# Two counters and one type: step weights of a hot pass (2 to 4), a layer's pacing point (0.88 to 0.94), and node keys in fp32

## The chip, the core and the metric

The kernel runs on one core of one Trainium2 chip. The core has five engines with a queue of instructions each, and each queue runs in order: PE (TensorE, matrix products), DVE (VectorE), ACT (ScalarE), POOL (GpSimd) and SP (SyncE, which here only issues transfers). An instruction that waits holds up everything behind it on its own engine and nothing else; engines meet at semaphores. SBUF is the working memory of 128 partitions, PSUM holds the results of products, and transfers between HBM and SBUF run on 16 DMA engines. The metric is the device time of one execution in microseconds (us).

## The reference, cut to what matters

There are 12,500 nodes with 256 numbers each and 200,000 edges, sorted by target. A graph convolution of three layers is followed by a feed-forward block on the half of the nodes that a router scores highest:

```
x = x + gcn(layernorm(x))          # three layers, gelu between them
x = x + ffn(layernorm(x))          # the top half of the rows

def _gcn_layer(x, src, dst, norm, W, b, n_nodes):
    h = x @ W
    msg = h[src] * norm[:, None]
    out = jax.ops.segment_sum(msg, dst, num_segments=n_nodes)
    return out + b
```

`dst` is 12500 u^2 with u uniform, so the low nodes have very many edges and the high ones few. The costly part of a layer is `segment_sum` of `h[src]`: 200,000 rows of 256 numbers picked by index.

## The kernel before, in words

**Blocks and tables.** The nodes stand in NB = 98 blocks of 128. The table of a layer holds each node's row as three bf16 parts side by side (PARTS x D = 768 numbers, 1536 bytes), which together have the precision of fp32.

**Two ways to sum.** The first blocks (12, 16 and 8 in the three layers) are "hot" and are done densely: a matrix of counts (how often source l feeds target j) times the whole table. All edges from there on are gathered: a group is four tiles of 128 edges. For each tile `sum_groups` issues one indirect DMA on POOL (L955), which fetches 128 table rows into a buffer `m`; there are 30 such buffers in layers 0 and 1, 20 in layer 2. DVE makes a one-hot matrix `oh` of the targets (L962), PE multiplies it with the rows (L968, twelve products a group), and two DVE instructions add the product in PSUM to a ring of block sums (L978, `here` and `there`). Layer 0 gathers 1027 tiles (257 groups), layer 1 943 (236 groups), layer 2 1127 (282 groups).

**Building the counts.** `build_counts(p)` makes the counts for the four target blocks of hot pass p and stores them to HBM. For each block w it lists the sources of each node by an indirect DMA on POOL (L1014), splits a source into its place and its block on DVE, turns both by a product, and keeps them as `keys` (L1059, written at L1049). Then it compares keys with constant rows: `low_h` (L1084, place, 128 values x up to 4 edges) and `high_h` (L1086, block, 98 or 196 values x up to 4 edges). The pair is multiplied on PE (L1053, "a count product"), and ACT copies the finished counts from PSUM (L1098). Blocks 5 and up are "paired": one instruction covers two edges of each node. Block 0 has more edges than the others and comes in 16 chunks; for its high columns the compares have one edge each (128x128 and 128x98), and they are few. `low_h` and `high_h` have 6 buffers in layer 0 and 3 in layer 1. Build 0 has 160 wide pairs of compares (128x512 with 128x392) and 62 narrow ones, build 1 has 32 with 128x392 and 48 with 128x784, builds 2 and 3 have 64 each with 128x784. Builds 0, 1 and 2 run in layer 0, build 3 in layer 1, none in layer 2.

**Multiplying the counts.** `hot_pass(i, p)` runs over the 98 table blocks; SP loads `t_row` (192 KB, L1128, 5 buffers) and every seventh block `t_cols` (896 KB, L1120, 2 buffers). For each block and each half of the columns three products of 128x512 are issued (L1132), and then the generator yields. There are 3, 4 and 2 passes in the three layers.

**What sets the order.** The instructions are written out by a loop over the groups, and the dense work is laid between them. After each tile of a group `sum_groups` calls `beside` (L1313 and on) with the share of the layer's groups that are done. `beside` takes steps from `all_parts` until the weights of the steps taken reach `share / 0.88` of the layer's whole `cost` (0.55 in layer 2). A step's weight is what the generator yields: 2 for a listing, 1 for a count product, 2 for three products of a pass:

```
                while done < min(1.0, share / (0.88 if i < 2 else 0.55)) * cost:
                    step = next(it, None)
                    if step is None:
                        break
                    done += step
```

`cost` adds `pass_cost = 4 * NB + 4 + WB` = 400 for each pass and `build_cost` for each build (742, 328, 264, 264), in layer 1 also 8 for a check of the order. `all_parts` runs build k beside pass k-1, in proportion to their costs; build 0 has no pass beside it, and the last pass of a layer no build. `beside` also advances the lane of finished rows (`go_on`, every second call): `next_rows` takes the sums of two blocks, applies the layer's end and the next layer's product (L795), and stores the next table. Rows that are left at the end of a layer follow after its last group, and the first gather of the next layer waits for their store.

Of the kernel before, what the change touches and what calls it, by code (L numbers as in the profile page):

```python
# [9 lines left out]
F32 = mybir.dt.float32  # L10
BF16 = mybir.dt.bfloat16
# [6 lines left out]
P = 128  # L18
# [4 lines left out]
NB = (N + P - 1) // P  # L23
# [27 lines left out]
WB = 4  # L51
# [41 lines left out]
def kernel(  # L93
# [911 lines left out]
    def build_counts(p, turn, work, keep, hot, unit, ps_u):  # L1005

        if True:
# [47 lines left out]
            for w in range(p * WB, (p + 1) * WB):  # L1055
                paired = w >= PAIRED
                chunks = CHUNKS if w == 0 else (U if paired else P,)
                first_col = [sum(chunks[:c]) for c in range(len(chunks))]
                keys = keep.tile([P, 2, sum(chunks)], BF16, name="keys0" if w == 0 else "keys", bufs=1 if w == 0 else 2)  # L1059
                for c, m in enumerate(chunks):  # L1060
                    listed(w, c, P if paired else m, keys[:, :, first_col[c] : first_col[c] + m])
                    yield 2
                per = 2 if paired else 1
                width = per * NB
                values = iota_2 if paired else iota_g
                for h in range(2):
                    a = unit.tile([P, NB, U], BF16, name="a")
                    for j in range(0, U, GT * per):
                        col = (h * U + j) // per
                        many = sum(m > col for m in chunks) > 4  # L1070
                        places = {}
                        for k0 in range(0, GT, GT // per):
                            pa = ps_u.tile([P, NB, 4], F32, name="pa")
                            for k in range(k0, k0 + GT // per):
                                if k not in places:
                                    most = 1 if many else GT
                                    for c, m in enumerate(chunks):
                                        n = min(most, m - col - k)
                                        if n <= 0:
                                            break  # L1080
                                        at = first_col[c] + col + k
                                        key = lambda q, v: keys[:, q, None, at : at + n].to_broadcast([P, v, n])
                                        low = hot.tile([P, P, GT], BF16, name="low_h")
                                        nc.vector.tensor_tensor(low[:, :, :n], key(0, P), iota_1[:, :, :n], OP.is_equal)  # L1084
                                        high = hot.tile([P, 2 * NB, GT], BF16, name="high_h")
                                        nc.vector.tensor_tensor(  # L1086
                                            high[:, :width, :n], key(1, width), values[:, :width, :n], OP.is_equal
                                        )
                                        for q in range(n):
                                            places.setdefault(k + q, []).append((low[:, :, q], high[:, :width, q]))  # L1090
                                        if many:
                                            one(pa, k - k0, per, places[k][-1], c == 0, col + k >= max(chunks[c + 1 :], default=0))
                                        yield 1 if many else 0
                                if not many:
                                    for c, hots in enumerate(places[k]):
                                        one(pa, k - k0, per, hots, c == 0, c == len(places[k]) - 1)
                                        yield 1
                            nc.scalar.copy(a[:, :, j + k0 * per : j + k0 * per + 4], pa)  # L1098
                            if len(places[k0]) > 2:
                                top = hot.tile([P, 1], F32, name="top")  # L1100
                                nc.vector.tensor_reduce(top, pa.rearrange("p n j -> p (n j)"), AX.X, OP.max)
                                nc.vector.scalar_tensor_tensor(
                                    bad[:, 6:7], top, 255.0, bad[:, 6:7], op0=OP.is_gt, op1=OP.max
                                )
                    nc.vector.tensor_tensor(a[:, w, :], a[:, w, :], ident[:, h * U : (h + 1) * U], OP.add)
                    nc.sync.dma_start(
                        counts[w // WB][:, :, w % WB * 2 + h, :].rearrange("c l x -> l c x"),
                        a.rearrange("p (c n) j -> p c (n j)", c=NS),
                    )

    def hot_pass(i, p, turn, dones, rows_p, cols_p, back, ps):

        if True:
            sums = [ps.tile([P, WB * P], F32, name=f"sum{h}") for h in range(2)]
            t_cols = {}

            def load(c):
                if c < NS:
                    t_cols[c] = cols_p.tile([P, 2 * WB, HB, U], BF16, name="t_cols")
                    nc.sync.dma_start(t_cols[c].rearrange("p u n j -> p u (n j)"), counts[p][c])  # L1120

            load(0)
            for c in range(NS):
                load(c + 1)
                for n in range(HB):
                    t_row = rows_p.tile([P, PARTS * D], BF16, name="t_row")
                    b = c * HB + n
                    nc.sync.dma_start(t_row, tables[i][b * P : (b + 1) * P, :])  # L1128
                    for h in range(2):
                        for part in range(PARTS):  # L1130
                            f = part * D + h * P
                            nc.tensor.matmul(  # L1132
                                sums[h], t_row[:, f : f + P], t_cols[c][:, :, n, :],
                                start=(b == 0 and part == 0), stop=(b == NB - 1 and part == PARTS - 1),
                            )
                        yield 2
            for h in range(2):
                turned = back.tile([P, WB * P], F32, name=f"turned{h}")
                nc.scalar.copy(turned, sums[h])
                sums[h] = turned  # L1140
                yield 2
            for k in range(0, WB, 2):
                pk = turn.tile([P, 2, DC, P], F32, name="pt")
                for j in range(2):
                    for h in range(2):
                        nc.tensor.transpose(pk[:, j, h, :], sums[h][:, (k + j) * P : (k + j + 1) * P], ident)
                done = dones.tile([P, 2, D], F32, name="done")
                nc.vector.tensor_copy(done.rearrange("p n d -> p (n d)"), pk.rearrange("p n c d -> p (n c d)"))
                yield 2
                yield (p * WB + k, 2, ("whole", done))  # L1150
# [60 lines left out]
    def layer(i):  # L1211
# [10 lines left out]
        with ExitStack() as s:  # L1222
            w = layer_weights(s, i)
# [9 lines left out]
            pools = layer_pools(h, (30, 30, 20)[i])  # L1233
            for_pass = pass_pools(h)
            for_build = build_pools(h, (6, 3)[i]) if made else None
            pass_cost = 4 * NB + 4 + WB

            def all_parts():

# [4 lines left out]
                while passes or builds:  # L1244
                    b = p = None
                    b_cost = p_cost = 0
                    if builds:
                        k, b_cost = builds.pop(0)
                        b = build_counts(k, mine[1], *for_build)
# [27 lines left out]
            cost = PASSES[i] * pass_cost + sum(build_cost(before_now + k) for k in range(made)) + (8 if i == 1 else 0)  # L1277
            it = all_parts()
            done = 0
# [33 lines left out]
            def beside(g, share):  # L1313
                nonlocal done, slot, junk_at
                if junk_at is not None and g >= junk_at:
                    junk_at = None
                    b0 = junk[0]
                    for b in range(b0, b0 + junk[1], 2):
                        clear(b, 2, ring)
                while done < min(1.0, share / (0.88 if i < 2 else 0.55)) * cost:  # L1320
                    step = next(it, None)
                    if step is None:
                        break
                    done += step
                slot += 1
                if i == 2 or slot % 2 == 0:
                    go_on(g)
                if i == 2 and (slot % 2 == 0 or len([x for x in ffns if not x[4]]) > 1):
                    ffn_on()
# [209 lines left out]
    with tc.tile_pool(name="flag", bufs=1) as work, tc.tile_pool(  # L1539
        name="ps_flag", bufs=1, space=bass.MemoryType.PSUM  # L1540
# [41 lines left out]
```

## Time and profile before

| what | value |
|---|---|
| median of 13 runs | 4653.12 us (4646.86 to 4667.55) |
| the profiled execution | 4652.44 us |
| its span, first to last instruction | 4650.5 us |
| PE busy | 3811.1 us (82%) |
| DVE busy | 2178.5 us (47%) |
| ACT busy | 1064.6 us (23%) |
| POOL busy | 3219.1 us (69%) |
| gathers of layer 0, first and last start | 235 to 1680 us |
| gathers of layer 1 | 1744 to 2960 us |
| gathers of layer 2 | 3015 to 4483 us |
| mean granted TensorE clock | 0.912 |

How to read it: a row of a group says line, engine, operation, output and inputs, shapes and the number of instructions, then the busy time in us and the mean of one in ns, and then the idle time of the engine just before them with what ended it. A view by stretches gives, for each stretch, the busy time of every engine with its number of instructions in brackets, then the granted TensorE clock, the busy share of the DMA engines and GB/s. Instructions of one engine overlap by some 75 ns where they follow each other at once, so sums of durations are a little above busy time.

### The profile page before, as it was taken

To read this page: it belongs to the slowest core of one execution; us is meant where nothing else is said; L and a number is where in the kernel's file an instruction comes from. 1 tells how busy PE (TensorE), PEld (TensorE's weight loads), DVE (VectorE), ACT (ScalarE), POOL (GpSimd) and SP (SyncE) were. 2 spreads that over 40 slices of the span, in tenths; PEclk is the share of its full clock that TensorE was granted. 3 is DMA by queue.
4 is the path that set the end of the run, shared out by engine and by line. 5 is a ranking of instruction groups with operands and counts; after the bars stand their busy time and mean duration, and the time that the engine had idled before them with its cause. 6 is when DMAs were issued, how large, how long until landed. Compare 5 with 4: busy or idle time off the path is not lost. (4 is left out here: it accounts for less than half of the span.)

```text
span 4650.5 us, 64287 instructions
## 1 busy us (share of the span) xinstructions
PE 3811.1 (82%) x21815; PEld 2731.4 (59%) x21815; DVE 2178.5 (47%) x5972; ACT 1064.6 (23%) x2187; POOL 3219.1 (69%) x3329
## 2 busy tenths in 40 slices
PE   5757669989798857888999988578999999888966
PEld 4635446656455544555556655345767778777755
DVE  8767545555443443444333334333343445455556
ACT  6602222333221121222111111201121113223311
POOL 4477777777766737777777777477776777777740
PEclk9968889999899978998999999789999999999978
DMA  5746678989898847899999998578877776666648
GB/s 165 256 124 183 211 234 302 325 292 337 292 323 298 267 147 251 284 294 322 337 324 338 334 320 262 157 233 253 261 240 232 257 247 196 194 198 198 200 130 295
DMA packets 591308, 1176.38 MB, mean 253 GB/s; under 512 B 78368, under 2 KB 403128, under 8 KB 590968
## 3 DMA queue, kind: packets, MB, share of 16 engines
q0 software_dynamic: 199200, 610.24, 42.5%
q1 hardware_dynamic: 285910, 460.42, 28.6%
q10 hardware_dynamic: 105858, 101.52, 6.6%
q8 instruction: 173, 2.83, 0.2%
q14 instruction: 167, 1.37, 0.1%
HBM read 988.29 MB, written 183.59 MB: 252 GB/s over the span
## 5 line engine op out<-in xcount | busy, mean ns | idle before, releaser
L955 POOL DMA_INDIRECT m<-table,idx x3097 | 3073.8, 992 | 1199.2 <-issue 440.8
L968 PE MATMUL pm<-m,oh 128*128 128x256 bf16 x9291 | 1503.8, 289 | 524.0 <-DMA m<-table,idx 380.9
L968 PEld LDWEIGHTS <-oh 128*128 128x128 bf16 x9291 | 1063.5, 117 | 958.8 <-issue 486.9
L1132 PE MATMUL sum<-t_cols,t_row 128*128 128x512 bf16 x5292 | 1464.5, 393 | 81.9 <-DMA t_row<-table 81.6
L978 DVE SCALAR_TENSOR_TENSOR ring<-pm,here,ring 128x256 f32 x775 | 373.0, 481 | 1812.1 <-PE pm L968 1697.5
L1132 PEld LDWEIGHTS <-t_row 128*128 128x128 bf16 x5292 | 533.8, 102 | 444.2 <-DMA t_row<-table 102.0
L1098 ACT CAST a<-pa 128x392 bf16<-128x392 f32 x512 | 246.3, 486 | 927.8 <-PE pa L1053 926.6
L902 PE MATMUL ph<-zt,w1t 128*128 128x256 f32 (+1 forms) x1600 | 403.1, 394 | 12.2 <-ACT ht L906 8.0
L1053 PE MATMUL pa<-high_h,low_h 128*128 128x98 bf16 (+1 forms) x1536 | 354.5, 318 | 43.1 <-DVE high_h L1086 35.0
L913 PE MATMUL py<-w2t,ht 128*128 128x256 f32 x1568 | 377.6, 382 | 5.4 <-DVE both L920 3.6
L978 DVE SCALAR_TENSOR_TENSOR ring<-pm,there,ring 128x256 f32 x775 | 368.9, 476 | 1.1
L962 DVE TENSOR_TENSOR oh<-lo,iota_g 128x512 bf16<-128x512 bf16 x775 | 320.8, 415 | 76.5 <-PE pm L968 76.3
L902 PEld LDWEIGHTS ph<-zt,w1t 128*128 128x128 f32 x1600 | 293.8, 199 | 79.9 <-ACT ht L906 27.5
L795 PE MATMUL ph<-gw,zt 128*128 128x256 f32 x1176 | 304.1, 405 | 19.3 <-DVE zt L788 9.4
L913 PEld LDWEIGHTS py<-w2t,ht 128*128 128x128 f32 x1568 | 288.7, 191 | 44.8 <-DVE both L920 3.8
L906 ACT ACTIVATE ht<-ph,b1t 128x256 f32<-128x256 f32 (+1 forms) x400 | 183.0, 468 | 415.4 <-PE ph L902 373.9
L795 PEld LDWEIGHTS ph<-gw,zt 128*128 128x128 f32 x1176 | 229.9, 203 | 68.1 <-ACT parts L810 8.8
L1053 PEld LDWEIGHTS <-low_h 128*128 128x128 bf16 x1536 | 174.2, 123 | 112.2 <-DVE low_h L1084 25.5
L1084 DVE TENSOR_TENSOR low_h<-keys,iota 128x512 bf16<-128x512 bf16 (+1 forms) x431 | 183.2, 425 | 84.8 <-PE pa L1053 84.3
L780 ACT ACTIVATE z<-z 128x512 f32<-128x512 f32 (+1 forms) x100 | 62.3, 623 | 631.3 <-DVE z L776 630.9
L868 ACT ACT_TABLE_LOAD x45 | 57.7, 1283 | 575.0 <-DVE mv L866 261.3
L801 ACT ACTIVATE own<-ph,dis 128x256 f32<-128x256 f32 x294 | 124.3, 469 | 274.9 <-PE ph L795 246.6
(272 smaller groups left out, 2243.6 us busy)
## 6 DMA issues: line engine op xcount, KB each, us to landing
t_row<-table SPq DMA_DIRECT2D x882, 192.0 KB
t_cols<-counts SPq DMA_DIRECT2D x126, 896.0 KB
table<-parts SPq DMA_DIRECT2D x144, 384.0 KB
counts<-a SPq DMA_DIRECT2D x32, 1568.0 KB
m<-table,idx POOLq DMA_INDIRECT x3097, 4.3
own<-own ACTq DMA_DIRECT2D x144, 256.0 KB
own_row<-own ACTq DMA_DIRECT2D x126, 256.0 KB
ys<-both SPq DMA_DIRECT2D x44, 512.0 KB
```

The costliest lines, as they stand in the source:

```text
L795: nc.tensor.matmul(ph[:, j, :], zt[:, j, c, :], w["w"][:, c, :], start=(c == 0), stop=(c == DC - 1))
L902: nc.tensor.matmul(ph[:, k - k0, : n * P], w["1"][:, c, k * P : (k + 1) * P], zt[:, c, :n, :], start=(c == 0), stop=(c == DC - 1),)
L906: nc.scalar.activation(ht[:, k, : n * P], ph[:, k - k0, : n * P], AF.Gelu_apprx_tanh, bias=w["b1"][:, k : k + 1])
L913: nc.tensor.matmul(py[:, j, :], ht[:, k, j * P : (j + 1) * P], w["2"][:, k, :], start=(k == 0), stop=(k == HK - 1))
L955: nc.gpsimd.indirect_dma_start(out=m[j], out_offset=None, in_=tables[i], in_offset=bass.IndirectOffsetOnAxis(ap=idx[:, u + j : u + j + 1], ...
L962: nc.vector.tensor_tensor(oh, lo[:, None, u : u + GT].to_broadcast([P, P, GT]), iota_g, OP.is_equal)
L968: nc.tensor.matmul(pm, oh[:, :, j], m[j][:, k * D : (k + 1) * D], start=(j == 0 and k == 0), stop=(j == tiles - 1 and k == PARTS - 1),)
L978: nc.vector.scalar_tensor_tensor(sums, pm, mask[:, g : g + 1], sums, op0=OP.mult, op1=OP.add)
L1053: nc.tensor.matmul(pa[:, :, k * per : (k + 1) * per], low, high, start=start, stop=stop)
L1084: nc.vector.tensor_tensor(low[:, :, :n], key(0, P), iota_1[:, :, :n], OP.is_equal)
L1098: nc.scalar.copy(a[:, :, j + k0 * per : j + k0 * per + 4], pa)
L1132: nc.tensor.matmul(sums[h], t_row[:, f : f + P], t_cols[c][:, :, n, :], start=(b == 0 and part == 0), stop=(b == NB - 1 and part == PARTS ...
```

## The change

The keys become fp32. A step of a pass weighs 4 instead of 2 in `beside` and in the proportion of builds to passes; the cost of a pass is written to match (8 x 98 + 8 = 792; it was 400). The pacing point of layers 0 and 1 goes from 0.88 to 0.94 of the groups. No instruction is added or removed; the compares at L1084 and L1086 read fp32 where they read bf16, and L1049 writes fp32. The keys take 2560 bytes a partition instead of 1280 for block 0, and 1024 instead of 512 for each of two buffers of the others.

```
-                keys = keep.tile([P, 2, sum(chunks)], BF16, name="keys0" if w == 0 else "keys", bufs=1 if w == 0 else 2)
+                keys = keep.tile([P, 2, sum(chunks)], F32, name="keys0" if w == 0 else "keys", bufs=1 if w == 0 else 2)
...
                                 sums[h], t_row[:, f : f + P], t_cols[c][:, :, n, :],
                                 start=(b == 0 and part == 0), stop=(b == NB - 1 and part == PARTS - 1),
                             )
-                        yield 2
+                        yield 4
...
-            pass_cost = 4 * NB + 4 + WB
+            pass_cost = 8 * NB + 4 + WB
...
-                while done < min(1.0, share / (0.88 if i < 2 else 0.55)) * cost:
+                while done < min(1.0, share / (0.94 if i < 2 else 0.55)) * cost:
```

## The prediction

> **What bounds the kernel now.** I read the groups by cost first, then the view by stretches, then the timeline of POOL and DVE where a gather is long. The costliest group is the gather, and the first two gathers of the timeline show its pace.
>
> ```profile
> L955 POOL DMA_INDIRECT m<-table,idx x3097 | 3073.8, 992 | 1199.2 <-issue 440.8
> ...
> 371.19 0.96 POOL L955 DMA_INDIRECT m<-table,idx  x1 [0.30 <-PE pm L968]
> 372.46 0.94 POOL L955 DMA_INDIRECT m<-table,idx  x1 [0.30 <-issue]
> 373.71 0.94 POOL L955 DMA_INDIRECT m<-table,idx  x1 [0.30 <-issue]
> 374.95 4.76 POOL L955 DMA_INDIRECT m<-table,idx  x1 [0.30 <-PE pt L785]
> ```
>
> An undisturbed gather takes 0.95 us and the next begins 0.30 us later: one each 1.25 us. 3097 of them need 3871 us of the 4650.5 us span. The rest is the start (235 us), two joints between layers (63 and 54 us), the end, and what the gathers lose. So each stretch is read as "POOL instructions times 1.25 against its length".
>
> ```profile
> 300.00:400.00 100.00, 71.31 (x503) 56.23 (x504) 88.07 (x289) 15.56 (x30) 78.17 (x72) 0.84 0.57 163
> 664.00:985.00 321.00, 284.61 (x1719) 192.19 (x1717) 156.15 (x405) 86.33 (x176) 247.07 (x243) 0.93 0.91 301
> 985.00:1270.00 285.00, 238.53 (x1391) 161.12 (x1389) 141.47 (x343) 82.34 (x167) 220.11 (x214) 0.91 0.93 315
> 1300.00:1600.00 300.00, 265.67 (x1530) 168.72 (x1528) 114.36 (x258) 48.75 (x92) 198.47 (x201) 0.97 0.91 308
> 1757.00:2130.00 373.00, 297.29 (x1705) 195.66 (x1703) 161.20 (x388) 76.01 (x154) 284.68 (x289) 0.91 0.85 276
> 2130.00:2700.00 570.00, 525.61 (x3041) 335.68 (x3042) 207.93 (x474) 80.91 (x148) 434.73 (x443) 0.97 0.96 332
> ```
>
> Columns three to seven are PE, weight loads, DVE, ACT, POOL. Build 0 runs in 300:400 with DVE 88% busy and POOL losing 10%. In 1300:1600, the last pass of layer 0, 201 gathers need 251 us of 300: 49 us lost, behind PE (89% busy, gathers wait for `m` to come free) and DMA (0.91). Passes of layer 1 lose only 16 us of 570 (443 gathers). So PE limits in one place only, and POOL everywhere else.
>
> What stretches a gather is on DVE. The gather at 374.95 ends at 379.71; DVE then:
>
> ```profile
> 374.11 0.47 DVE L978 SCALAR_TENSOR_TENSOR ring<-pm,there,ring 128x256 f32 x1
> 374.50 0.41 DVE L1084 TENSOR_TENSOR low_h<-keys,iota 128x512 bf16<-128x512 bf16 x1
> 374.84 0.35 DVE L1086 TENSOR_TENSOR high_h<-keys,iota_g 128x392 bf16<-128x392 bf16 x1
> ...
> 378.49 0.41 DVE L962 TENSOR_TENSOR oh<-lo,iota_g 128x512 bf16<-128x512 bf16 x1
> 378.82 0.47 DVE L978 SCALAR_TENSOR_TENSOR ring<-pm,here,ring 128x256 f32 x1
> ```
>
> From 374.50 to 378.9 DVE runs compares without a break, all with two inputs in SBUF, and the gather gets on only when a ring addition (one input in PSUM) follows. In 985:1270, a gather takes 1.03 us on average. The compares of the counts thus cost POOL time as well as DVE time.
>
> **Price of fp32 keys.** Rows by form:
>
> ```profile
> L1084 DVE TENSOR_TENSOR low_h<-keys,iota 128x512 bf16<-128x512 bf16 x368 | 153.6, 417 | 84.8 <-PE pa L1053 84.3
> L812 DVE TENSOR_TENSOR parts<-rest,parts 128x512 bf16<-128x512 f32 x144 | 99.5, 691 | 39.8 <-ACT parts L810 39.5
> L1086 DVE TENSOR_TENSOR high_h<-keys,iota 128x784 bf16<-128x784 bf16 x176 | 98.1, 557 | 0.0
> L861 DVE TENSOR_TENSOR both<-t,xt 128x256 f32<-128x256 f32 x98 | 40.7, 415 | 1.2
> L1086 DVE TENSOR_TENSOR high_h<-keys,iota_g 128x392 bf16<-128x392 bf16 x192 | 67.5, 352 | 0.0
> ```
>
> L812 has one fp32 and one bf16 input and a bf16 output, as the compares will have: 0.69 us for 512 elements against 0.42. The line through L861 and L812 (1.05 ns an element) gives, undisturbed, 0.68 us for 512, 0.56 for 392, 0.97 for 784. The wide compares grow by 0.266, 0.206 and 0.41 us. Per build: build 0 160 x 0.472 = 75.5 us; build 1 32 x 0.472 + 48 x 0.676 = 48 us; builds 2 and 3 64 x 0.676 = 43 us each; 210 us of DVE. The narrow compares (0.47 and 0.41 us for 128 and 98 elements) already run slowly and I leave them; if they too grew, 62 pairs at 0.1 us would be 6 us. L1049 reads PSUM in fp32 already: nothing, at most 31 x 0.1 = 3 us.
>
> **Price of the weights.** Layer 0: build 0 took 742/2534 x 0.88 x 257 = 66 groups, now 742/3710 x 0.94 x 257 = 48. Pass 0 with build 1 goes from 65 to 73 groups, pass 1 with build 2 from 59 to 69, pass 2 from 36 to 52. Layer 1: pass 0 with build 3 from 74 to 68 groups, each further pass from 44 to 51. Layer 2 keeps its proportions: no change, give or take 3 us. SP's `t_row`, `t_cols` and count stores move with their steps, ACT's count copies (0.49 us each) with the builds, POOL's 31 listings forward; ACT is under 30% busy in all these stretches, and SP's queue keeps its kind of order. The next thing late on PE is the gather's product behind a count product whose compare is not ready; behind it the ring additions, `m` buffers and so POOL.
>
> **The sum, layer 0.**
>
> 1. Build 0 (groups 0 to 48). Before, DVE is busy 201 us in 235:545, by when 118 of the 160 wide pairs are done. Through group 48 after: 201 + 42 more pairs x 0.61 (start to start) + 75.5 + some 5 before 235 and in listings = 307 us. POOL needs 194 gathers and 21 listings x 1.25 = 269 us plus what compares take. Before, POOL was past 195 gathers after 290 us (235:525). Low end: DVE never idle from 228 on, +20. High end: the two additions of a group let two gathers in and the other two come only when DVE stands still, 307 + 48 x 2 x 1.25 = 427 us, +137. Nearest row: 300:400, the densest build, with DVE 88% busy: 307/0.88 = 349 us, **+59**.
> 2. Builds 1 and 2. In 664:1270 gathers average 1.017 to 1.034 us, 0.07 to 0.09 over 0.95: 36 us over 448 gathers. About half of the two-input DVE time is compares: 18 us. A compare 1.65 times as long costs 1.65 times (+12) if each delay stays as it is, or 1.65 squared (+31) if a gather meets it more often and waits longer each time. I take nearer the second, as L1084's chains have no gaps: **+25**.
> 3. Pass 2 spread over 52 groups: 98 x 6 / 52 = 11.3 dense products a group where layer 1 carried 13.2 (588/44) at a loss of 3%. The 49 us lost in 1300:1600 falls to about 9: **-40**; if the late end of pass 2 costs some of it, -10; if nothing is lost, -49.
> 4. The joint after layer 0 (63 us): the order of both programs leaves seven pairs of rows (28 products L795) at groups 250 and on in either: **0**, or +8 for one more pair (63 us / 7 = 9).
>
> Layer 1: build 3 in 1757:2130 stretches gathers by 289 x 0.04 = 12 us, a third of it compares: +3 to +8, **+7** as it is also denser. Less dense later passes: of 16 us lost in 570, **-2** (0 to -6).
>
> 59 + 25 - 40 + 0 + 7 - 2 = +49, on the profiled 4652.4 us (0.7 us below the median, so no correction): **4701 us**.
>
> A rule of the Trainium skill weighs here: SBUF — State Buffer, "Who interferes with whom", says that a DVE instruction with two SBUF inputs holds up only GpSimd work that reads SBUF, and infers that tensor_tensor leaves descriptor generation alone. The gather of 4.76 us above contradicts the second half for gathers with an index in SBUF. By the inference, items 2 and build 3's +7 would go and the sum would be 4669 us.
>
> **Rivals.** *Main case*, gathers and DVE in each other's way in build 0, part repaid in pass 2: 0.68, 4670 to 4760. *Serialised*: in build 0 gathers pass only between compare chains; for it speaks the gather at 374.95, against it the 10% loss at 88% DVE; item 1 at its high end, 4701 + 78 = 4779: 0.15. *Faster*: the wide compares keep 0.42 us on fp32 keys (the change does not make DVE longer). Then DVE needs 232 us in build 0 and POOL 269 / 0.89 = 302 (+12), item 2 and the +7 vanish, the pass gives -42: 4622. L812's row speaks against it; it decides if L1084's mean stays under 0.5 us: 0.10. *Even*: item 1 at +20, item 2 at +12, +3, -40: about 4647 to 4660: 0.07.
>
> **Numbers.** Within 0.2% (9 us, about what a measurement tells from no change) are the even case less what of it falls faster: 0.05. Faster 0.11, slower 0.84. Range: 4658, leaving out the faster cases, to 4795, a little over the serialised case.
>
> **What would show it.** L1084 at 512 and L1086 at 784 with means near 0.68 and 0.97 us; the first L1132 earlier in groups but about the same time (664 us) or later; POOL's gathers in build 0 well over 1.1 us; DVE at 85% or more there; 1300:1700 back at some 77 gathers in 100 us; the third layer 1468 us long as before. Wrong if build 0 never makes DVE the bound, if PE's start of pass 0 (it waits for `t_cols`) stalls longer with full `m` buffers (each 10 us counts whole), or if row lanes pile up at a joint.

## The result and the profile after

The changed kernel takes 4727.0 us (median of 8 runs, 4719.4 to 4738.5) against 4654.5 us before (37 runs): 1.0156 times as long, with a 95% interval of 1.0143 to 1.0169. The profiled execution has a span of 4728.7 us, 78.2 us more than before. Forecast was 4701 us, slower, in a range of 4658 to 4795: sign and range held, and the size was short by some 26 us.

The compares first. These are the rows by form of the changed kernel:

```profile
L1084 DVE TENSOR_TENSOR low_h<-keys,iota 128x512 bf16<-128x512 f32 x368 | 251.3, 683 | 46.4 <-PE pa L1053 46.3
L1086 DVE TENSOR_TENSOR high_h<-keys,iota 128x784 bf16<-128x784 f32 x176 | 169.9, 966 | 0.0
L1086 DVE TENSOR_TENSOR high_h<-keys,iota_g 128x392 bf16<-128x392 f32 x192 | 106.9, 557 | 0.0
L1084 DVE TENSOR_TENSOR low_h<-keys,iota 128x128 bf16<-128x128 f32 x62 | 29.9, 483 | 0.0
```

683, 966 and 557 ns were forecast as 680, 970 and 560, and the narrow form stays where it was (483 ns against 472). DVE is 203 us busier over the span (2381.8 against 2178.5); the forecast was 210.

The groups and the stretches of the changed kernel:

```profile
L955 POOL DMA_INDIRECT m<-table,idx x3097 | 3172.3, 1024 | 1178.5 <-issue 443.4
...
300.00:400.00 100.00, 65.58 (x371) 45.98 (x371) 91.33 (x240) 10.22 (x21) 65.85 (x55) 0.72 0.42 121
400.00:500.00 100.00, 70.28 (x460) 53.18 (x458) 91.27 (x197) 30.40 (x61) 83.55 (x55) 0.81 0.56 171
1400.00:1700.00 300.00, 250.47 (x1449) 162.90 (x1448) 115.29 (x261) 43.20 (x79) 225.88 (x228) 0.92 0.92 311
2210.00:2780.00 570.00, 505.63 (x2921) 326.20 (x2919) 210.45 (x479) 80.94 (x148) 435.56 (x442) 0.96 0.94 317
```

In build 0 only 55 POOL instructions fall in 300:400, where it was 72, and DVE is 91% busy. In the last pass of layer 0 (1400:1700 now, 1300:1600 before) there are 226 gathers in 300 us (the row's 228 POOL instructions hold two listings), where it was 201. So one place lost and the other won, as forecast. This is what a gather in build 0 looks like now, POOL first and then DVE under the second of these gathers:

```profile
387.62 0.94 POOL L955 DMA_INDIRECT m<-table,idx  x1 [0.30 <-issue]
388.87 4.36 POOL L955 DMA_INDIRECT m<-table,idx  x1 [0.30 <-issue]
393.54 5.13 POOL L955 DMA_INDIRECT m<-table,idx  x1 [0.31 <-PE pa L1053]
398.97 5.13 POOL L955 DMA_INDIRECT m<-table,idx  x1 [0.30 <-PE pa L1053]
```

```profile
387.62 0.47 DVE L978 SCALAR_TENSOR_TENSOR ring<-pm,there,ring 128x256 f32 x1
388.02 0.68 DVE L1084 TENSOR_TENSOR low_h<-keys,iota 128x512 bf16<-128x512 f32 x1
388.62 0.56 DVE L1086 TENSOR_TENSOR high_h<-keys,iota_g 128x392 bf16<-128x392 f32 x1
...
391.86 0.56 DVE L1086 TENSOR_TENSOR high_h<-keys,iota_g 128x392 bf16<-128x392 f32 x1
392.33 0.47 DVE L978 SCALAR_TENSOR_TENSOR ring<-pm,here,ring 128x256 f32 x1
```

Four pairs of compares follow each other from 388.02 to 392.42, then come two ring additions with a one-hot compare between them; the gather that began at 388.87 ends at 393.23. For three gathers in a row one gets through per chain.

Since POOL sets the pace, the simplest account of a run is the time from the start of one gather to the start of a later one, taken from the trace. "Order" to "two inputs" are the experiments below.

| gathers | holds | before | after | keys | order | one input | two inputs |
|---|---|---|---|---|---|---|---|
| 1st to 195th | most of build 0 | 288.9 | 358.7 | 320.3 | 308.4 | 313.1 | 396.1 |
| 195th to 765th | builds 1, 2, passes 0, 1 | 776.7 | 806.2 | 830.0 | 768.6 | 779.4 | 814.3 |
| 765th to 1027th | pass 2 | 378.8 | 346.0 | 384.5 | 346.9 | 341.1 | 344.1 |
| joint | rows left over | 64.0 | 69.1 | 67.8 | 67.8 | 64.6 | 65.5 |
| first 273 of layer 1 | build 3 | 353.1 | 363.6 | 365.5 | 350.3 | 352.7 | 351.3 |
| rest of layer 1 | passes | 863.3 | 863.1 | 860.8 | 859.2 | 857.2 | 856.9 |
| layer 2 | | 1466.6 | 1468.4 | 1468.2 | 1465.2 | 1470.4 | 1468.0 |

Besides, each run has a figure that I call stretch: what its gathers take above 946 ns, summed over those that take more. It is 23 us in the first 194 gathers of the kernel before and 72 in the changed one, 47 and 82 in the next 570, 11 and 22 in the first 273 of layer 1.

### The profile page after: what moved, and what is told of

It reads as the page before. It is cut to its first block, busy times and chain, and to the rows that moved or that the text cites. A ratio compares the mean times of both kernels' runs of the same rounds, so it can differ in the third digit from the quotient of the medians.

```text
span 4728.7 us, 64315 instructions
## 1 busy us (share of the span) xinstructions
PE 3844.3 (81%) x21815; PEld 2733.7 (58%) x21815; DVE 2381.8 (50%) x5972; ACT 1065.8 (23%) x2187; POOL 3320.0 (70%) x3329
## 5 line engine op out<-in xcount | busy, mean ns | idle before, releaser
L955 POOL DMA_INDIRECT m<-table,idx x3097 | 3172.3, 1024 | 1178.5 <-issue 443.4
L968 PE MATMUL pm<-m,oh 128*128 128x256 bf16 x9291 | 1500.4, 290 | 532.2 <-DMA m<-table,idx 429.9
L968 PEld LDWEIGHTS <-oh 128*128 128x128 bf16 x9291 | 1065.0, 118 | 1002.4 <-issue 508.7
L1132 PE MATMUL sum<-t_cols,t_row 128*128 128x512 bf16 x5292 | 1498.2, 396 | 48.5 <-DMA t_row<-table 43.5
L1132 PEld LDWEIGHTS <-t_row 128*128 128x128 bf16 x5292 | 540.6, 103 | 393.4 <-issue 56.4
L1053 PE MATMUL pa<-high_h,low_h 128*128 128x98 bf16 (+1 forms) x1536 | 344.7, 325 | 93.5 <-DVE high_h L1086 77.7
L1084 DVE TENSOR_TENSOR low_h<-keys,iota 128x512 bf16<-128x512 f32 (+1 forms) x431 | 281.6, 653 | 46.4 <-PE pa L1053 46.3
```

The costliest lines, as they stand in the source:

```text
L955: nc.gpsimd.indirect_dma_start(out=m[j], out_offset=None, in_=tables[i], in_offset=bass.IndirectOffsetOnAxis(ap=idx[:, u + j : u + j + 1], ...
L968: nc.tensor.matmul(pm, oh[:, :, j], m[j][:, k * D : (k + 1) * D], start=(j == 0 and k == 0), stop=(j == tiles - 1 and k == PARTS - 1),)
L1053: nc.tensor.matmul(pa[:, :, k * per : (k + 1) * per], low, high, start=start, stop=stop)
L1132: nc.tensor.matmul(sums[h], t_row[:, f : f + P], t_cols[c][:, :, n, :], start=(b == 0 and part == 0), stop=(b == NB - 1 and part == PARTS ...
```

## The experiments

Theory A: instructions with two inputs in SBUF hold the gathers, and fp32 makes them longer. Rival B: DVE's time as such is what costs, since count products, PE and the `m` buffers wait for it. Rival C: the crowded build 0 of the new order is what costs. Four kernels ran side by side, with the kernel before at 4659 us.

**fp32 keys alone**, in the places of before:

```
-                keys = keep.tile([P, 2, sum(chunks)], BF16, ...
+                keys = keep.tile([P, 2, sum(chunks)], F32, ...
```

> The kernel before with fp32 keys alone; weights 2 and pacing point 0.88 stay. Theory A (the longer compares, all with two inputs in SBUF, hold gathers back): the first 194 gathers take 289 us before and 359 after the whole change; with build 0 still spread over 66 groups I expect 289 + 45, builds 1 and 2 +30 as in the whole change, the last pass of layer 0 unchanged, layer 1 +10: 4653 + 85 = 4738, or 4725 to 4750, slower than the whole change or level with it. Rival C (the new places are what costs, keys do not): 4655 to 4670.

Measured 4754.2 us, 1.0207 (1.0187 to 1.0227): a little above the range of theory A (4725 to 4750), and more than the whole change (1.0156). The first 194 gathers pay 31 us, not 45, since build 0 reaches on to gather 264; the next stretch pays 53.

**The order alone**, the whole change with bf16 keys:

```
-                        yield 2
+                        yield 4
-            pass_cost = 4 * NB + 4 + WB
+            pass_cost = 8 * NB + 4 + WB
-                while done < min(1.0, share / (0.88 if i < 2 else 0.55)) * cost:
+                while done < min(1.0, share / (0.94 if i < 2 else 0.55)) * cost:
```

> The whole change with bf16 keys: weights 4 and pacing point 0.94 alone. Theory A: the first 194 gathers 289 to 305 us, builds 1 and 2 about level, the stretch of the last pass of layer 0 33 us shorter, the joint +5: 4653 - 20 = 4633, or 4620 to 4645, faster than both kernels. Rival C (the crowding of build 0 is what costs): the first 194 gathers 340 us or more, and 4670 to 4720.

Measured 4621.6 us, 0.9925 (0.9906 to 0.9944), in the range of theory A, though two of its parts missed: the first 194 gathers take 308.4 us where 289 to 305 was expected, and builds 1 and 2 gain 8 where they were to be level. Rival C falls on this chip. Pass 2 gains 32 us and the first 194 gathers lose 19.5, of which stretch is only 5 (28 us against 23). Of the rest, the listings take some 6 us more (POOL runs 21 of them in that time, before 19), and POOL stands still some 8 us longer before gathers.

**The same DVE time, with one input in SBUF.** The order alone, and behind each wide compare a reduction whose result is not used:

```
+  if n > 1:
+      fill = hot.tile([P, 1], F32, name="fill", bufs=2)
+      nc.vector.tensor_reduce(fill, <iota_1, flat>[:, :192], AX.X, OP.max)        # behind low
+      nc.vector.tensor_reduce(fill, <iota_2, flat>[:, : 328 if paired else 130], AX.X, OP.max)   # behind high
```

> As the run on the order alone, and behind each wide compare a reduction with one input in SBUF, of 192 elements behind the place compare and of 130 or 328 behind the block compare. That gives DVE about the added time of fp32 keys (0.27, 0.20 and 0.41 us) in instructions with one SBUF input; it computes nothing that is used. Theory A (gathers are held by instructions with two SBUF inputs): gathers stay at about 1.0 us in builds; DVE is as busy as after the change, which alone makes the first 194 gathers 310 to 330 us; in all 4653 to 4690. Rival B (only DVE's time counts, whatever it does): equal to the whole change, 4715 to 4740.

**The same DVE time, with two inputs in SBUF.**

```
+  if n > 1:
+      fill = hot.tile([P, 656], BF16, name="fill", bufs=1)
+      of = <iota_1, flat>[:, :384]                               # behind low
+      of = <iota_2, flat>[:, : 656 if paired else 260]           # behind high
+      nc.vector.tensor_tensor(fill[:, :n_of], of, of, OP.is_equal)
```

> As the run before this, but the filler behind each wide compare is a comparison of two bf16 inputs in SBUF (384 elements, 260 or 656), of the same DVE time; nothing of it is used. Theory A and rival B both: like the whole change, 4715 to 4745, with mean gathers in build 0 above 1.3 us. If it comes out with the one-input filler instead, below 4700, neither holds for the added time and it is the fp32 read itself that costs.

Measured 4639.1 us with one input, 0.9968 (0.9957 to 0.9979), and 4747.2 us with two, 1.0188 (1.0165 to 1.0211). Theory A's total for one input, 4653 to 4690, was too high, and two inputs lie just above 4715 to 4745. The fillers are a match in number and length; first the kernel with one input, then the one with two:

```profile
L1087 DVE TENSOR_REDUCE fill<-iota 128x1 f32<-128x192 bf16 x369 | 126.3, 342 | 0.0
L1094 DVE TENSOR_REDUCE fill<-iota 128x1 f32<-128x328 bf16 x176 | 85.0, 483 | 0.0
L1094 DVE TENSOR_REDUCE fill<-iota 128x1 f32<-128x130 bf16 x193 | 53.7, 278 | 0.0
```

```profile
L1088 DVE TENSOR_TENSOR fill<-iota 128x384 bf16<-128x384 bf16 x369 | 130.2, 353 | 1.4
L1096 DVE TENSOR_TENSOR fill<-iota 128x656 bf16<-128x656 bf16 x176 | 87.0, 494 | 1.6
L1096 DVE TENSOR_TENSOR fill<-iota 128x260 bf16<-128x260 bf16 x193 | 55.9, 290 | 0.0
```

DVE is busy for 2377.9 us with one input, 2391.7 with two, and 2381.8 in the changed kernel. In all, the fillers cost 17.5 us over the order alone in the first form and 125.6 in the second; fp32 keys cost 105. But these totals do not compare like with like, for the fillers did not all run where the kernel's text has them. A filler reads only constants, and nothing reads its result. The time of the fillers on DVE by stretches, first with one input, then with two (behind the length of a stretch stand DVE's busy time with them and their number):

```profile
232.00:546.00 314.00, 82.56 (x268) 0.73 0.55 163
546.00:950.00 404.00, 111.75 (x342) 0.92 0.86 282
950.00:1300.00 350.00, 0.00 (x0) 0.94 0.91 307
1300.00:1420.00 120.00, 44.60 (x128) 0.91 0.95 317
1420.00:2100.00 680.00, 0.00 (x0) 0.90 0.82 269
```

```profile
232.00:628.00 396.00, 102.00 (x318) 0.70 0.45 134
628.00:1400.00 772.00, 115.88 (x291) 0.91 0.85 277
1450.00:1600.00 150.00, 54.59 (x128) 0.92 0.95 314
1600.00:2210.00 610.00, 0.00 (x0) 0.91 0.82 271
```

In build 0 either kernel runs two fillers for each wide pair: 322 in all, nearly each directly behind its compare or one instruction later. With one input, the 64 wide pairs of 950:1300 have no filler beside them, where with two inputs the 61 pairs of that window have 122. And in both kernels the 128 fillers of build 3 run in pass 2 of layer 0, where there is no compare, and none in layer 1. So the fair comparison is build 0, the first row of the table above: over the order alone the first 194 gathers pay 5 us with one input (313.1 against 308.4), 88 with two (396.1) and 50 with fp32 keys (358.7). Since the two-input fillers are bf16, it is not the reading of fp32 that costs. Rival B is left with 5 us there; what one-input work costs beside the compares of builds 1 to 3 was not measured. The gathers of build 0 show where the rest lies. Groups of POOL in build 0, in this order the kernel with one input (232 to 546 us), with two (232 to 628), and the changed kernel (232 to 592):

```profile
L955 POOL DMA_INDIRECT m<-table,idx x195 | 201.1, 1031 | 148.9 <-DVE valid_l L1039 61.4 <-PE pm L968 42.0 <-issue 30.2
```

```profile
L955 POOL DMA_INDIRECT m<-table,idx x194 | 292.9, 1510 | 134.7 <-DVE valid_l L1039 60.4 <-issue 35.6 <-PE pm L968 23.7
```

```profile
L955 POOL DMA_INDIRECT m<-table,idx x195 | 257.3, 1319 | 137.3 <-DVE limit_l L1038 60.4 <-issue 34.1 <-PE pm L968 21.7
```

A gather takes 1031 ns beside one-input fillers with DVE 91 to 92% busy, less than the 1067 of the kernel before (its first 195) and the 1090 of the order alone: the fillers stand between the compares of a chain. This is one such gather, and DVE under it:

```profile
381.75 1.11 POOL L955 DMA_INDIRECT m<-table,idx  x1 [0.31 <-issue]
```

```profile
381.69 0.35 DVE L1089 TENSOR_TENSOR high_h<-keys,iota_g 128x392 bf16<-128x392 bf16 x1
381.95 0.28 DVE L1094 TENSOR_REDUCE fill<-iota 128x1 f32<-128x130 bf16 x1
382.15 0.41 DVE L1084 TENSOR_TENSOR low_h<-keys,iota 128x512 bf16<-128x512 bf16 x1
382.48 0.34 DVE L1087 TENSOR_REDUCE fill<-iota 128x1 f32<-128x192 bf16 x1
```

A gather takes 1510 ns beside two-input fillers. The fillers differ in one thing more: a two-input one writes 260 to 656 numbers, a reduction one. Writing is not what holds: in the kernel before, 243 gathers have ring additions on DVE for over 0.6 us of their first 0.945, and they take 0.948 us on average, although each addition writes 256 fp32 numbers to SBUF.

Two things follow from where the fillers ran. At the start of layer 1 the two-input fillers cost 1 us over the order (351.3 against 350.3), where fp32 keys cost 13 (363.6): no filler ran there, and stretch is 10 us where fp32 keys make 22. And the 128 two-input fillers in pass 2, 54.6 us of DVE, cost nothing that shows (344.1 us against 346.9): two-input instructions follow each other without a gap for 0.53 us there on average, less than one gather. What was not traced is why two-input fillers stretch the first 194 gathers by 37 us more than fp32 keys do (109 against 72), though a pair takes 1.08 us in either.

**On other chips.** The next runs were on three chips where the kernel before takes 5407 to 5473 us. Their ratios hold only beside the kernel before on the same chip, and what was expected in microseconds for a chip with 4655 us was not tested by them.

The pacing point alone, `share / 0.94` in the kernel before:

> The kernel before with the pacing point at 0.94 instead of 0.88 and nothing else. Build 0 then has 71 groups instead of 66 and the last pass of layer 0 38 instead of 36, so if the gain of the order (33 us) comes from a thinner last pass, a small part of it: 4640 to 4653. If the gain comes from the later end itself: 4620 to 4630.

Weights alone (4, pass cost to match, pacing point 0.88), twice:

> The kernel before with steps of a pass weighed 4 and the pass cost to match, pacing point 0.88, bf16 keys. Build 0 has 45 groups, the last pass of layer 0 48 instead of 36. If a thinner last pass is the gain: most of it, 4620 to 4637. If the later end is: 4645 to 4665, as build 0 is more crowded still.

> The same kernel as the run on weights alone (weights 4, pass cost to match, pacing point 0.88, bf16 keys), since that call met a chip on which the kernel before takes 5416 us. On a chip with the kernel before near 4655 us: a thinner last pass as the gain gives 4620 to 4640; the later end as the gain gives 4645 to 4665. On a chip near 5416 us: 1.007 of the kernel before, as there.

Weight 3 with `pass_cost = 6 * NB + 4 + WB` and 0.94:

> Steps of a pass weighed 3, pacing point 0.94, bf16 keys: build 0 has 57 groups and the last pass of layer 0 46. Against the order of the change (48 and 52 groups, 4622 us) build 0 loses some 10 us less, and the last pass at 12.8 dense products a group stays just under the 13.2 that layer 1 carried: 4612 to 4625. If the last pass comes back behind PE: 4630 to 4645.

The order alone and the whole change once more:

> The same kernel as the run on the order alone (weights 4, pacing point 0.94, bf16 keys), to complete the set of both, neither and each alone. On a chip with the kernel before near 4655 us: 4622 again, 0.9925. On a chip on which it takes 5416 or 5473 us: weights alone gave 1.004 and 1.007 there, the pacing point alone 0.999. If the two add up, 1.003 to 1.006; if the early crowding costs there because a gather's landing is what is waited for, the order is no gain there and beats nothing.

> The whole change on the same chip as the order alone, so that the price of the keys is had there: 105 us on a chip with the kernel before near 4655 us. On a slower chip, where gathers lose time to something else as well, part of what the compares hold is hidden: 50 to 100 us over the order alone, with the stretch of gathers in builds as long as on the other chip (72 us in the first 194 gathers, 83 in the next 570).

fp32 keys in build 0 alone (`F32 if p == 0 else BF16`) in the new places, twice:

> The whole change, with fp32 keys in build 0 alone and bf16 in builds 1 to 3. The order alone gave 4622 us and the whole change 4727, so the keys cost 105 us in the new places. The stretches of the two profiles share them as 50 us in the first 194 gathers, 38 in the next 570 and 13 at the start of layer 1. If every build's compares hold the gathers of their own stretch: 4622 + 50, and what of build 0 falls behind gather 194, so 4665 to 4685. If the cost sits in the crowded build 0 alone: 4715 or more.

> The same kernel as the run with fp32 keys in build 0 alone and the places of the whole change. On a chip with the kernel before near 4655 us: 4665 to 4685 if each build's compares hold the gathers of their own stretch, 4715 or more if all of the cost is in build 0. On a chip near 5416 us: 1.013 of the kernel before, as there.

Times are medians; the ratio is an estimate of its own from all runs and differs from that of the medians by up to 0.2%.

| kernel | before there, us | us | ratio (95%) |
|---|---|---|---|
| pacing point alone | 5416.0 | 5417.0 | 0.9993 (0.9966 to 1.0020) |
| weights alone | 5416.0 | 5452.6 | 1.0071 (1.0043 to 1.0098) |
| weights alone, again | 5473.3 | 5493.4 | 1.0041 (1.0022 to 1.0059) |
| weight 3 and 0.94 | 5416.0 | 5427.2 | 1.0017 (0.9988 to 1.0046) |
| order alone | 5406.8 | 5443.7 | 1.0048 (1.0017 to 1.0079) |
| whole change | 5406.8 | 5473.2 | 1.0120 (1.0055 to 1.0185) |
| keys in build 0 | 5416.0 | 5481.4 | 1.0129 (1.0087 to 1.0172) |
| keys in build 0, again | 5473.3 | 5528.8 | 1.0086 (1.0059 to 1.0113) |

The whole change is slower there too. For the repeats 1.007 and 1.013 were expected, a little more than came; the 1.003 to 1.006 for the order alone held. The order alone, a gain of 0.75% on the first chip, is a loss of 0.5% here. The keys cost 29 us by the medians (5473.2 - 5443.7) and 39 by the ratios, with an interval from about nothing to twice that, not 105 and not the 50 to 100 that was expected. In the two profiles all of it lies in the first 194 gathers (379.5 us against 340.4). In the next 570 fp32 keys add 25 us of stretch there too, and the time is level (898.8 against 896.3): POOL has other waits in which this hides. A stretch of layer 1 without builds shows why gains change, first the order on the first chip, then on such a chip:

```profile
2210.00:2780.00 570.00, 504.70 (x2907) 324.93 (x2906) 209.46 (x477) 79.73 (x146) 434.89 (x444) 0.96 0.93 313
```

```profile
2210.00:2780.00 570.00, 448.56 (x2463) 286.31 (x2461) 193.68 (x452) 84.27 (x164) 369.36 (x379) 0.91 0.82 269
```

Only 379 gathers start there in 570 us, a pace of 1.50 us and not 1.28, with a mean of 977 ns a gather on POOL against 981. So the gathers themselves are no longer; POOL stands still between them. The waits of the order on such a chip ("remote" stands where no instruction in the profile is the releaser):

```profile
PEld L968 <- issue: 721.9, 496, 21.7
POOL m L955 <- PE pm L968: 699.2, 607, 11.2
DVE ring L978 <- remote: 642.4, 112, 25.5
```

On the first chip POOL waits 272.0 us for an `m` buffer to come free of PE (699.2 here), and PE's weight loads 502.2 us for nothing that the profile shows. The products themselves are hardly longer (295 ns against 286 for L968, 402 against 396 for L1132). What holds PE up on these chips was not found.

The weights with keys of bf16 cannot be split from the pacing point for the first chip, as neither ran alone on it; on the others weights alone lose 37 and 20 us, the pacing point nothing that can be measured. That the cost of the keys is paid where the build runs shows in the stretch of these runs, which is of like size on either kind of chip (72, 82 and 22 us for the whole change on the first chip): with fp32 in build 0 alone it is 54 and 67 us, in the two runs, in the first 194 gathers, 50 in the next 570 and 10 and 9 in the first 273 of layer 1; with fp32 everywhere 59, 72 and 19; with bf16 22, 46 and 11. In time, the first 194 gathers take 375.2 and 379.5 us with keys in build 0, 379.5 with keys everywhere and 340.4 with the order alone. The totals of these two runs (65 and 55 us over the kernel before) are of other chips than the rest and do not split finer.

## Why the prediction was right, and where it was short

The sign, the main case and the paces that it named held: gathers at 1.25 us set the time, the wide compares grew as L812's row said, the last pass of layer 0 got its gathers back (226 in 300 us, 75 in 100 where 77 was forecast), layer 2 stayed within 2 us (1466.6 before, 1468.4 after), DVE was 89 to 91% busy from 300 to 600 us. One sign was misjudged: the first dense product came at 620 us, not at 664 or later, as build 0 has fewer groups to wait for.

By its steps, in the two profiles:

- **Item 1, build 0**, +59: measured +69.8. The order alone gives 19.5 of it and the keys 50.3. The size was near by luck, for the reason was not: it divided DVE's work by an 88% occupancy, as if DVE's time were the limit. DVE's time does set where build 0 ends: its last wide place compare starts at 539 us with the order alone, at 587 with one-input fillers and at 597 in the changed kernel. But POOL runs up to 30 `m` buffers ahead of that, and the kernel with one-input fillers, whose build 0 ends nearly as late, passes the 195th gather after 313.1 us, not 358.7. What limits the gathers is the hold. The steps that failed are "POOL needs 194 gathers and 21 listings x 1.25 = 269 us plus what compares take", left without a number, and the choice of the row 300:400 for it. Its low end does not follow either: 307 us of DVE without a pause from 228 on end at 535, 300 us after 235, which is +10 and not +20. The serialised rival had the right picture of a single chain (the timeline above) and a price of 137 us, twice too high, because not all gathers of build 0 meet a chain: their mean is 1319 ns, where a gather that meets one takes up to 5 us.
- **Item 2, builds 1 and 2**, +25: +29.5. The order alone saves 8.1 and the keys cost 37.6, above the high end of +31 that was given for them.
- **Item 3, pass 2**, -40: -32.8. The loss fell from 51 to 18 us (262 gathers at 1.251 us), not to 9; the order alone has 19.
- **Item 4, the joint**, 0: +5.1, though the seven pairs of rows are the same. It lies between 64.6 and 69.1 us in the five runs on the first chip with changed kernels. In SP's queue the last store of the table stands behind loads of `t_row` and `t_cols`; that this is what varies was not shown.
- **Build 3**, +7: +10.5. Rest of layer 1, -2: -0.2. Layer 2, 0: +1.8.

The terms sum to +84 and the start, the second joint and the end give back 6. So 11 of the missing 29 us are build 0, 7 pass 2, and 3 to 5 each the joint, builds 1 and 2 and build 3. The two errors of size on the keys have one sign: a hold was priced from the length of one compare, while the timelines show gathers waiting for the end of a whole chain. For builds 1 and 2 it was not separated whether this or the share of 18 us taken for the compares was too small.

The 4622 us of the faster rival are what the order alone took (4621.6), but its terms were not: +12, 0 and -42 were forecast for build 0, builds 1 and 2 and pass 2, and +19.5, -8.1 and -31.9 measured. That they cancel is luck.

The point where the skill was weighed is decided too: had two-input instructions left the gathers alone, the forecast would have been 4669 us. In build 0, where the two fillers ran in the same places, they leave the first 194 gathers 83 us apart. So the measurement stands against the inference that the Trainium skill's SBUF — State Buffer makes in "Who interferes with whom" for tensor_tensor, and with its rule for GpSimd work that reads SBUF.

## What to carry to other kernels

Where POOL issues indirect transfers back to back, price a DVE instruction by the number of its SBUF inputs and by what stands behind it, not by its length alone: in build 0 some 0.1 ms more DVE work cost the gathers 5 us with one input and 88 us with two. A filler that nothing depends on can run elsewhere than the kernel's text has it, so see in the trace where it ran before comparing totals. A dtype that takes a two-input compare from 0.42 to 0.68 us is paid on POOL, and a one-input instruction between compares lets a gather through. A gain of under 1% from placing work can turn over on another chip of the same kind, so run it on more than one.

## What the runs showed of the hardware that was not expected

- A gather is held for a whole chain of DVE instructions with two SBUF inputs, up to 6.41 us in the changed kernel where it takes 0.95 alone, and goes on when one with a PSUM input or with a single SBUF input follows. Reductions of 192 and 130 elements (342 and 278 ns, one SBUF input) between compares are enough: with them gathers in build 0 average 1031 ns although DVE does more.
- Narrow compares that write every fourth element (128x128) take 472 ns with bf16 keys and 483 with fp32: these hardly get longer.
- The same kernel takes 4654 us on one chip and 5407 to 5473 us on others, where the mean granted TensorE clock is 0.87 and not 0.91, the gather itself is as long, and POOL and PE stand still more. The cause was not settled.
